# Layer 0's input transpose: from TensorE to a blocked load and a VectorE transpose

## The chip, the cores and the metric

The kernel runs on one core of one Trainium2 chip. The metric is device time in microseconds (us), and less is better. The core's engines are PE (TensorE, matrix multiplies and transposes), DVE (VectorE), ACT (ScalarE), POOL (GpSimd) and SP (SyncE, which here only issues DMAs). Each engine works through its own queue in order.

## The reference

64 graphs of 256 nodes with 256 features each pass through four graph layers; each layer's output is added to its input and normalised. In layer 0, which the change touches, x has the shape (64, 256, 256):

```python
q = proj(Wq, bq); k = proj(Wk, bk); v = proj(Wv, bv)     # x @ W.T + b, four heads of 64
attn = softmax(where(adj == 0, NEG, q @ k.T * 64 ** -0.5))
out = layer_norm((attn @ v) @ Wo.T + bo) * gamma + beta
x = layernorm(x + out)
```

Layer 1 is a second attention (eight heads of 32) with an MLP of width 1,024, layer 2 a graph attention with a rank-one score, and layer 3 a softmax over x * a0 @ x.T. All is computed in float32.

## The kernel before

The 64 graphs are worked on in 32 groups of two (G = 2, so T = 512 nodes, in TB = 4 blocks of 128 partitions). A group is a generator, `group(g)`, that issues some instructions and yields, about 45 times in all. A string, ORDER, says which group takes the next turn: in each of 32 periods the newest group takes its first turn, and older groups (up to five periods old) take theirs in between, so several groups at different layers are in work at once. FIRST and LAST are the same for the start and the end of the run. The program's order is made binding on PE alone (`in_order`); on the other engines a scheduler places instructions by when it expects their inputs, so an instruction there can move ahead of the turn that issued it.

The parts that matter here:

- `load_group(g)` issues two DMAs of 512 KB on SP, one for x (buffer `x0`, three buffers) and one for the integer adjacency `adj` (two buffers).
- `group(g)` casts `adj` to bf16 on ACT (L889), has four DMA transposes turn it (L897), and makes the mask on DVE (L900). `adjb`, the cast copy, has one buffer, so the next group's cast waits for this mask.
- `layer0` begins with `transposed(x)` (L577): for each of two halves of the features, four PE transposes of 128x128 (L531) go into one PSUM tile, and ACT copies it to `xT` (L584). Then PE computes q and k (`xT` as the moving operand) and v.
- `layer0` then has POOL add `beta0` to x in place (L717), because x is next needed in x + beta0. As it overwrites x, it waits for the PE transposes that read x. The sum is read at L744.
- `behind` in `layer0` normalises each graph twice. `stats` (L536) is a chain of DVE statistics (L544, L545), POOL additions (L547, L549) and a POOL power (L551). With `twice=True` two small DVE products follow (L553, L554). `scaled` (L557) then makes `z` on DVE (L559), once for each block of 128 nodes. In the instruction order they stand L553, L559 (first block of the graph), L554, L559 (second block), then L750, which makes `xb`.
- `layer1` starts with PE transposes of `z` (L758, again through L531), and multiplies exp(scores) by the mask on DVE, 32 instructions for each group (L613).

Tiles named `xT` share three buffers among five uses for each group. PSUM tiles named `pm` have four.

Of the kernel before, what the change touches and what calls it, by code (L numbers as in the profile page):

```python
# [8 lines left out]
F32 = mybir.dt.float32  # L9
BF16 = mybir.dt.bfloat16  # L10
I32 = mybir.dt.int32
# [5 lines left out]
P = 128  # L17
N = 256
D = 256
NC = D // P  # L20
G = 2
QB = N // P
TB = G * QB
T = G * N
# [376 lines left out]
def usual_input(ctx: ExitStack, tc: tile.TileContext, a: dict, out: bass.AP, flag: bass.AP):  # L401
# [7 lines left out]
    nc = tc.nc  # L409
# [3 lines left out]
    io = ctx.enter_context(tc.tile_pool(name="io", bufs=2))  # L413
    act = ctx.enter_context(tc.tile_pool(name="act", bufs=AT_ONCE))
# [24 lines left out]
    r_3 = const.tile([P, B // G, TB], F32, name="r_3")  # L439
    last = const.tile([P, B // G, TB], F32, name="last")  # L440

    def load_group(g):
        x0 = io.tile([P, TB, D], F32, name="x0", bufs=3)
        nc.sync.dma_start(x0, a["x"][g * G:(g + 1) * G].rearrange("b (q p) d -> p (b q) d", p=P))
        adj = io.tile([P, TB, N], I32, name="adj")
        nc.sync.dma_start(adj, a["adj"][g * G:(g + 1) * G].rearrange("b (q p) k -> p (b q) k", p=P))
        return x0, adj

    later = []

# [6 lines left out]
    def load_rows(name, cols, queue=None):  # L457

        src = a[name]
        t = const.tile([P, src.shape[0] // P, cols], F32, name=name)  # L460
        load(queue, t, src.rearrange("(c p) f -> p c f", p=P))
        return t
# [13 lines left out]
        return t  # L476


    first = load_group(0)
    wqT = load_rows("L0_gnn_WqT", D, nc.scalar)  # L480
    wkT = load_rows("L0_gnn_WkT", D, nc.scalar)
    bq = load_column(a["L0_gnn_bq"], D, "bq", nc.scalar)
# [44 lines left out]
    def matmul(*args, **kw):  # L527
        in_order(nc.tensor.matmul(*args, **kw))  # L528
# [38 lines left out]
    def tokens(gs):  # L567
        return slice(gs[0] * N, (gs[-1] + 1) * N)

    def to_psum(src, c, gs=ALL):  # L570

        pt = ps_m.tile([P, T], F32, name="pm")
        for t in blocks_of(gs):
            transpose(pt[:, t * P:(t + 1) * P], src[:, t, c * P:(c + 1) * P], ident)
        return pt

    def transposed(src, scale=None, bias=None, gs=ALL):  # L577

        on = tokens(gs)
        dst = act.tile([P, NC, T], F32, name="xT")  # L580
        for c in range(NC):
            pt = to_psum(src, c, gs)
            if scale is None:
                nc.scalar.copy(dst[:, c, on], pt[:, on])  # L584
            else:
                nc.scalar.activation(dst[:, c, on], pt[:, on], AF.Identity, bias=bias[:, c:c + 1], scale=scale[:, c:c + 1])  # L586
        return dst
# [92 lines left out]
    def project(dst, srcT, w, extra, row=None, gs=ALL):  # L680


        chunks = w.shape[1]
        for i in gs:
            pm = ps_m.tile([P, QB, D], F32, name="pm")
            if row is not None:
                matmul(pm, onesb, row.unsqueeze(1).to_broadcast([P, QB, D]), start=True, stop=False)
            for q in range(QB):
                t = i * QB + q
                for c in range(chunks):  # L690
                    matmul(pm[:, q, :], srcT[:, c, t * P:(t + 1) * P], w[:, c, :],
                           start=c == 0 and row is None, stop=c == chunks - 1 and (row is None or q == QB - 1))
                if chunks > NC:
                    yield
            o = dst[:, i * QB:(i + 1) * QB, :]
            if extra is None:
                nc.scalar.copy(o, pm)
            else:
                nc.vector.tensor_tensor(o, pm, extra[:, i * QB:(i + 1) * QB, 0:D], ALU.add)

    def layer0(g, x, mask):
        xT = transposed(x)
        yield
        qT = act.tile([P, NC, T], F32, name="qT")
        kT = act.tile([P, NC, T], F32, name="kT")
        for w, bcol, dst in ((wqT, bq, qT), (wkT, bk, kT)):
            for f in range(NC):
                pm = ps_m.tile([P, T], F32, name="pm")
                for c in range(NC):
                    matmul(pm, w[:, c, f * P:(f + 1) * P], xT[:, c, :], start=c == 0, stop=c == NC - 1)  # L710
                nc.scalar.activation(dst[:, f, :], pm, AF.Identity, bias=bcol[:, f:f + 1])
            yield
        v = act.tile([P, TB, D], F32, name="v")
        yield from project(v, xT, wvT, None)
        yield

        nc.gpsimd.tensor_tensor(x, x, over_blocks(beta0), ALU.add)  # L717
        y = act.tile([P, TB, D], F32, name="y")
        z = act.tile([P, TB, D], F32, name="z")
        xb = act.tile([P, TB, D], F32, name="xb", tag="v")  # L720

        def behind(i, oT, rz):

            rr = att.tile([P, NC, N], F32, name="rr")
            lines = dram.tile([NC, 2, N], F32, name="lines")

            queue = nc.sync if g else nc.gpsimd
            queue.dma_start(lines.rearrange("c h n -> (c h) n"), rz[0:P:32, :])
            for h in range(2):
                queue.dma_start(rr[h * 64:h * 64 + 64, :, :], lines[:, h, :].unsqueeze(0).to_broadcast([64, NC, N]))  # L730
            yield
            nc.vector.tensor_tensor(oT, oT, rr, ALU.mult)  # L732
            yield
            pm = ps_m.tile([P, QB, D], F32, name="pm")
            for q in range(QB):
                for c in range(NC):
                    matmul(pm[:, q, :], oT[:, c, q * P:(q + 1) * P], woT[:, c, :],
                           start=c == 0, stop=c == NC - 1)
            nc.vector.tensor_tensor(y[:, i * QB:(i + 1) * QB, :], pm, over_blocks(bop, QB), ALU.add)
            yield  # L740
            mv, rstd = stats(y, i)
            for q, t in enumerate(blocks(i)):
                nc.vector.scalar_tensor_tensor(y[:, t, :], y[:, t, :], mv[:, q, 0:1], gamma0, ALU.subtract, ALU.mult)  # L743
                nc.vector.scalar_tensor_tensor(y[:, t, :], y[:, t, :], rstd[:, 0, q:q + 1], x[:, t, :],  # L744
                                               ALU.mult, ALU.add)
            yield
            mv, rstd = stats(y, i, twice=True)
            scaled(z, y, i, mv, rstd[:, 1])
            for q, t in enumerate(blocks(i)):
                nc.vector.scalar_tensor_tensor(xb[:, t, :], z[:, t, :], rstd[:, 0, q:q + 1], beta1r, ALU.mult, ALU.add)  # L750
            yield

        yield from attention(qT, kT, v, mask, 64, None, behind, [r_0[:, g * G + i:g * G + i + 1] for i in range(G)])
        return xb, z
# [128 lines left out]
        return (yield from values_of(lambda i, kc, q: e[:, i, at[kc][q]:at[kc][q] + P], x, D, x, r_3[:, g], gs, last[:, g]))  # L883

    def group(g):
        x, adj = load_group(g) if g else first
        yield
        adjb = io.tile([P, TB, N], BF16, name="adjb", bufs=1)
        nc.scalar.activation(adjb, adj, AF.Copy, accum_out=there[:, g:g + 1])  # L889
        nc.scalar.activation(adj.bitcast(F32), adj, AF.Square, bias=minus_half, accum_out=edges[:, g:g + 1])  # L890
        yield


        pt = io.tile([P, G, QB, N], BF16, name="adjT", bufs=1)
        for t in range(TB):
            i, q = divmod(t, QB)
            nc.sync.dma_start_transpose(pt[:, i, :, q * P:(q + 1) * P], adjb[:, t, :])  # L897
        yield
        mask = act.tile([P, G, QB * N], BF16, name="mask")
        nc.vector.scalar_tensor_tensor(mask.rearrange("p g k -> p (g k)"), pt.rearrange("p g k q -> p (g k q)"), 1.0,  # L900
                                       adjb.rearrange("p t k -> p (t k)"), ALU.mult, ALU.min,
                                       accum_out=both_ways[:, g:g + 1])
        xb, z = yield from layer0(g, x, mask)
        y, hT, both = yield from layer1(xb, z, mask)

        def others(gs):

            yield from project(y, hT, w2, both, b2m, gs)
            x = yield from renormed(y, gs)
            x = yield from layer2(x, mask, gs)  # L910
            x = yield from layer3(g, x, mask, gs)
            i, j = g * G + gs[0], g * G + gs[-1] + 1
            nc.sync.dma_start(out[i:j].rearrange("b (q p) d -> p (b q) d", p=P), x[:, gs[0] * QB:(gs[-1] + 1) * QB, 0:D])

        if g < B // G - 1:
            yield from others(ALL)
            return

        parts = [others((i,)) for i in ALL]
        turn = 0  # L920
        while parts:
            for r in parts[:turn // QB + 1]:
                if next(r, END) == END:
                    parts.remove(r)
            turn += 1
            yield
# [77 lines left out]
    for period in range(len(groups)):  # L1004
        for age in ORDER:
            g = period - int(age)
# [61 lines left out]
```

## Time and profile before

| | |
|---|---|
| median of 3 runs | 2663.03 us (2661.43 to 2664.4) |
| profiled execution, first to last instruction (span) | 2658.2 us |
| PE busy | 2586.9 us, 97% of the span |
| DVE busy | 1965.7 us, 74% |
| ACT busy | 1293.9 us, 49% |
| POOL busy | 592.3 us, 22% |
| DMA queue of SP (q1) | 111,552 packets, 78.94 MB, 10.1% of 16 engines' span |

The profiled execution gives its span only, and no launch-to-end time of its own: the median of the runs lies 4.8 us above the span, and the profiled execution is read as a run of that length. Busy times of PE are modelled, and neighbouring matmuls overlap in them, so the time that a group of matmuls takes is read from start to start. In the lists of instructions below, columns are the start in us from the beginning of the span, the duration in us, engine, line, operation, output and inputs, shapes, and the count; a bracket gives the engine's idle time before it and what ended that.

### The profile page before, as it was taken

What the parts mean: (1) busy time and instruction counts of PE and PEld (TensorE: products, weight loads), DVE (VectorE), ACT (ScalarE), POOL (GpSimd) and SP (SyncE); (2) the same over time, 40 slices, a digit from 0 to 9 for tenths busy, and PEclk for the clock granted to TensorE, in tenths of its full rate; (3) what the DMA queues carried; (4) which work ended last, traced back from release to release, by engine and by line L of the source; (5) the groups of instructions that cost most, each with busy time, mean ns of one, the idle gap of its engine ahead of it and who ended that gap; (6) DMA issues with size and microseconds to landing.
All of it is one profiled execution on the core that took longest, in us unless ns stands there. A gap on an engine that the chain in (4) does not pass through costs nothing.

```text
span 2658.2 us, 44921 instructions
## 1 busy us (share of the span) xinstructions
PE 2586.9 (97%) x16648; PEld 1761.5 (66%) x16648; DVE 1965.7 (74%) x6189; ACT 1293.9 (49%) x1997; POOL 592.3 (22%) x1145
## 2 busy tenths in 40 slices
PE   6899999999999999999999999999999999999996
PEld 3567667666667666666676666676676676676665
DVE  4667777777777777777777777777777777777774
ACT  3445544545545545545455544555445455445442
POOL 2112222222222222222222222222222222222121
PEclk8999999999999999999999999999999999999998
DMA  6001011001010000010010110110110101000000
GB/s 163 25 9 32 26 37 37 25 29 29 29 37 29 33 29 28 29 37 27 28 36 25 33 37 25 29 37 21 36 37 25 29 29 29 29 21 17 17 1 25
DMA packets 113393, 83.20 MB, mean 31 GB/s; under 512 B 44304, under 2 KB 112656, under 8 KB 113168
## 3 DMA queue, kind: packets, MB, share of 16 engines
q1 hardware_dynamic: 111552, 78.94, 10.1%
q8 instruction: 134, 2.20, 0.4%
q10 hardware_dynamic: 1360, 0.79, 0.1%
q0 software_dynamic: 256, 0.53, 0.1%
q14 instruction: 91, 0.75, 0.1%
HBM read 54.80 MB, written 17.04 MB: 27 GB/s over the span
## 4 chain that ended last, share of the span: by engine, by line
PE 71%; DVE 17%; POOL 9%; issue 2%; DMA 1%; ACT 0%; SPq 0%; DVEq 0%; POOLq 0%; ACTq 0%
PE pm L528 55%; PE ps L528 10%; PE pm L531 7%; POOL rstd L551 6%; DVE st L544 3%; DVE y L816 2%; DVE y L744 2%; DVE xn L559 2%; POOL ve L547 2%; DVE z L559 2%; DVE mv L545 1%; DVE xb L750 1%; DVE y L743 1%; DVE r L815 1%; POOL ve L549 0%
## 5 line engine op out<-in xcount | busy, mean ns | idle before, releaser
L613 DVE SCALAR_TENSOR_TENSOR e<-e,mask 128x256 f32<-128x256 f32 x1024 | 428.2, 483 | 130.7 <-ACT e L605 130.7
L605 ACT ACTIVATE e<-ps 128x1024 f32<-128x1024 f32 x384 | 371.9, 1020 | 196.2 <-PE ps L528 176.3
L528 PE MATMUL pm<-L_gnn_W,hT 128*128 128x256 f32 x2048 | 463.0, 379 | 0.0
L528 PE MATMUL pm<-xT,L_gnn_W 128*128 128x512 f32 x1024 | 455.2, 592 | 0.0
L528 PEld LDWEIGHTS pm<-L_gnn_W,hT 128*128 128x128 f32 x2048 | 384.5, 190 | 49.2 <-issue 0.7
L788 ACT ACTIVATE hT<-pm,b 128x512 f32<-128x512 f32 x256 | 176.7, 691 | 408.1 <-PE pm L528 408.0
L528 PEld LDWEIGHTS pm<-xT,L_gnn_W 128*128 128x128 f32 x1024 | 191.7, 190 | 203.4 <-issue 198.5
L544 DVE BATCH_NORM_STATS2 st<-y 128x6 f32<-128x256 f32 x768 | 301.1, 408 | 6.7
L551 POOL TENSOR_TENSOR rstd<-ve,mhalf 128x2 f32<-128x2 f32 (+1 forms) x384 | 298.4, 777 | 26.7
L559 DVE TENSOR_SCALAR xn<-y,mv,rstd 128x256 f32<-128x256 f32 x384 | 141.9, 411 | 178.9 <-POOL rstd L551 178.8
L547 POOL TENSOR_SCALAR ve<-mv 128x2 f32<-128x2 f32 x384 | 98.9, 257 | 741.0 <-DVE mv L545 738.8
L774 POOL TENSOR_TENSOR both<-y,xb 128x512 f32<-128x512 f32 x64 | 81.4, 1272 | 764.2 <-DVE y L773 764.2
L607 DVE TENSOR_TENSOR e<-e,mask 128x1024 f32<-128x1024 f32 x128 | 150.8, 1221 | 15.3 <-ACT e L605 15.3
L528 PE MATMUL ps<-xT 32*128 32x256 f32 x2048 | 148.0, 402 | 2.2 <-ACT e L605 1.3
L586 ACT ACTIVATE xT<-pm,beta,gamma 128x512 f32<-128x512 f32 x128 | 92.3, 770 | 104.4 <-PE pm L531 104.3
L528 PE MATMUL pm<-e,z 128*32 128x256 f32 x2048 | 142.4, 387 | 0.3
L528 PEld LDWEIGHTS ps<-xT 32*128 32x128 f32 x2048 | 93.2, 185 | 74.0 <-issue 66.8
L528 PE MATMUL pm<-e,v 128*32 128x256 f32 x2048 | 125.4, 384 | 8.0 <-DVE e L607 8.0
L528 PE MATMUL pm<-L_gnn_WoT,oT 128*128 128x256 f32 x512 | 121.2, 391 | 8.3 <-DVE oT L732 6.0
L528 PE MATMUL ps<-qT,kT 64*128 64x256 f32 x1024 | 128.0, 389 | 0.5 <-ACT e L605 0.5
L528 PE MATMUL pm<-xT,L_gnn_WqT 128*128 128x512 f32 x256 | 120.9, 616 | 3.7 <-ACT xT L584 3.7
L816 DVE SCALAR_TENSOR_TENSOR y<-pm,r,xn 128x256 f32<-128x256 f32 x256 | 120.9, 473 | 2.5
(138 smaller groups left out, 4059.1 us busy)
## 6 DMA issues: line engine op xcount, KB each, us to landing
x<-in_x SPq DMA_DIRECT2D x32, 512.0 KB
adj<-in_adj SPq DMA_DIRECT2D x32, 512.0 KB
rr<-lines SPq DMA_DIRECT2D x124, 128.0 KB
out<-xn SPq DMA_DIRECT2D x31, 512.0 KB
adjT<-adjb SPq DMA_TRANSPOSE x128
L_gnn_W<-in_L_gnn_W SPq DMA_DIRECT2D x2, 1024.0 KB
lines<-zs SPq DMA_DIRECT2D x62, 4.0 KB
rr<-lines POOLq DMA_DIRECT2D x4, 128.0 KB, 3.3
```

Source lines behind the costliest of these rows:

```text
L528: in_order(nc.tensor.matmul(*args, **kw))
L531: in_order(nc.tensor.transpose(*args))
L544: nc.vector.bn_stats(st[:, q, :], src[:, t, 0:D])
L547: nc.gpsimd.tensor_scalar(ve[:, 0], mv[:, :, 1], EPS, None, ALU.add)
L551: nc.gpsimd.tensor_tensor(rstd, ve, mhalf[:, 0:k * QB].rearrange("p (k t) -> p k t", k=k), ALU.pow)
L559: nc.vector.tensor_scalar(dst[:, t, 0:D], src[:, t, 0:D], mv[:, q, 0:1], rstd[:, q:q + 1], ALU.subtract, ALU.mult)
L586: nc.scalar.activation(dst[:, c, on], pt[:, on], AF.Identity, bias=bias[:, c:c + 1], scale=scale[:, c:c + 1])
L605: nc.scalar.activation(e, ps, AF.Exp, scale=scale)
L607: nc.vector.tensor_tensor(e, e, mask.unsqueeze(1).to_broadcast([P, 2, QB * N]), ALU.mult)
L613: nc.vector.scalar_tensor_tensor(e[:, h, k], e[:, h, k], 1.0, mask[:, k], ALU.mult, ALU.mult, accum_out=sums[:, kc, c, j:j + 1])
L788: nc.scalar.activation(hT[:, f, :], pm, AF.Gelu, bias=b1[:, f:f + 1])
L816: nc.vector.scalar_tensor_tensor(y[:, t, :], po[:, 0:D], r, x[:, t, 0:D], ALU.mult, ALU.add)
```

## The change

`load_group` is split in two. `load_edges(g)` loads `adj`, now with one buffer, at the place where `load_group` stood. `load_x(g)` is called later, after the DMA transposes of `adj`. It loads x as before (now two buffers), and a second time in 32x32 blocks, by eight DMAs into `turned`, such that a transpose of each 32x32 block within its place gives `xT`. One DVE instruction does this for the whole group (128 partitions x 1,024 elements). The eight PE transposes and the two ACT copies of layer 0 are gone. Line numbers behind the edit move by 10 to 12: L528 becomes L538, L551 becomes L561, L553 L563, L559 L569, L613 L623, L717 L728.

```diff
-    def load_group(g):
-        x0 = io.tile([P, TB, D], F32, name="x0", bufs=3)
+    def load_edges(g):
+        adj = io.tile([P, TB, N], I32, name="adj", bufs=1)
+        nc.sync.dma_start(adj, a["adj"][g * G:(g + 1) * G].rearrange("b (q p) k -> p (b q) k", p=P))
+        return adj
+
+    def load_x(g):
+        turned = io.tile([P, NC, T // 32, 32], F32, name="turned", bufs=1)
+        rows = a["x"][g * G:(g + 1) * G].rearrange("b n d -> (b n) d")
+        parts = rows.rearrange("(t i) (c k j) -> k i c t j", i=32, c=NC, j=32)
+        for k in range(P // 32):
+            for c in range(NC):
+                nc.sync.dma_start(turned[32 * k:32 * k + 32, c], parts[k, :, c])
+        x0 = io.tile([P, TB, D], F32, name="x0")
         nc.sync.dma_start(x0, a["x"][g * G:(g + 1) * G].rearrange("b (q p) d -> p (b q) d", p=P))
-        adj = io.tile([P, TB, N], I32, name="adj")
-        nc.sync.dma_start(adj, a["adj"][g * G:(g + 1) * G].rearrange("b (q p) k -> p (b q) k", p=P))
-        return x0, adj
+        return x0, turned
...
-    first = load_group(0)
+    first = load_edges(0), load_x(0)
...
-    def layer0(g, x, mask):
-        xT = transposed(x)
+    def layer0(g, x, turned, mask):
+        xT = act.tile([P, NC, T], F32, name="xT")
+        nc.vector.transpose(xT.rearrange("p c t -> p (c t)"), turned.rearrange("p c t j -> p (c t j)"))
...
-        x, adj = load_group(g) if g else first
+        adj = load_edges(g) if g else first[0]
...
             nc.sync.dma_start_transpose(pt[:, i, :, q * P:(q + 1) * P], adjb[:, t, :])
+        x, turned = load_x(g) if g else first[1]
         yield
...
-        xb, z = yield from layer0(g, x, mask)
+        xb, z = yield from layer0(g, x, turned, mask)
```

## The prediction

> **What bounds the kernel now.** I read the page's busy shares first, then its chain of waits, then PE's list of waits, then one period as timelines.
>
> ```profile
> PE 2586.9 (97%) x16648; PEld 1761.5 (66%) x16648; DVE 1965.7 (74%) x6189; ACT 1293.9 (49%) x1997; POOL 592.3 (22%) x1145
> ...
> PE 71%; DVE 17%; POOL 9%; issue 2%; DMA 1%; ACT 0%; SPq 0%; DVEq 0%; POOLq 0%; ACTq 0%
> ```
>
> ```profile
> PE pm L531 <- DVE z L559: 9.2, 30, 0.7
> ```
>
> PE is full, yet a quarter of the chain lies on DVE and POOL. The second block (PE's waits: us in total, times, longest) tells why: 30 times, once a period, PE waits about 0.3 us for `z`. A period is 80.33 us from mask to mask (L900 at 775.14 and 855.5). In the chain, PE works without a gap from 772.4 to 831.8 us; from there to 772.4 us of the next period DVE and POOL run statistics, powers and scalings up to `z`, while PE has other work for all but 0.3 us of it. So two things lengthen a period one for one: PE's work between 772 and 832, and any delay of `z`. Here is that place, PE first, then DVE and POOL.
>
> ```profile
> 771.37 0.38 PE L531 MATMUL pm<-ident,z 128*128 128x128 f32 x2
> 772.05 1.16 PE L531 MATMUL pm<-ident,z 128*128 128x128 f32 x6 [0.29 <-DVE z L559]
> ...
> 781.35 1.04 PE L531 MATMUL pm<-ident,x 128*128 128x128 f32 x8
> 782.22 3.62 PE L528 MATMUL pm<-L_gnn_W,hT 128*128 128x256 f32 x16
> ```
>
> ```profile
> 771.51 0.16 DVE L553 TENSOR_TENSOR rstd<-rstd 128x2 f32<-128x2 f32 x1 [1.71 <-POOL rstd L551]
> 771.59 0.41 DVE L559 TENSOR_SCALAR z<-y,mv,rstd 128x256 f32<-128x256 f32 x1
> 771.91 0.15 DVE L554 TENSOR_TENSOR rstd<-rstd,ve 128x2 f32<-128x2 f32 x1
> 771.98 0.41 DVE L559 TENSOR_SCALAR z<-y,mv,rstd 128x256 f32<-128x256 f32 x1
> ...
> 775.14 1.23 DVE L900 SCALAR_TENSOR_TENSOR mask<-adjT,adjb 128x1024 bf16<-128x1024 bf16 x1
> ...
> 782.26 0.42 DVE L613 SCALAR_TENSOR_TENSOR e<-e,mask 128x256 f32<-128x256 f32 x1
> ...
> 782.61 2.56 DVE L613 SCALAR_TENSOR_TENSOR e<-e,mask 128x256 f32<-128x256 f32 x1
> ```
>
> ```profile
> 770.45 1.03 POOL L551 TENSOR_TENSOR rstd<-ve,mhalf 128x4 f32<-128x4 f32 x1
> ...
> 782.47 2.42 POOL L717 TENSOR_TENSOR x<-x,beta 128x1024 f32<-128x1024 f32 x1 [2.97 <-PE pm L531]
> ```
>
> The eight transposes of x begin at 781.35 and the next matmul at 782.22: they hold PE for 0.87 us, not the 1.04 of the record. They lie in the stretch that is PE alone. At 782.61 the eighth masking instruction takes 2.56 us where its neighbours take 0.42: it starts during POOL's addition of `beta0` and ends just after it (782.47 + 2.42 = 784.89; 785.17). This is no single case. L613's mean over 1,024 instructions is 483 ns on the page and its median 421: 62 ns x 1,024 = 63 us, as if some 30 of them lost 2.1 us each, once a group. Today the loss is harmless: DVE is done with this graph's masking at 785.18, and PE starts on the values at 786.85.
>
> [...]
>
> **The change, part by part.** It can be followed in the order in which each engine's queue stands once the changed program is built.
>
> 1. *PE loses eight transposes a group.* Nothing else moves in its queue. 0.87 us a period, on the path, in about 30 periods (the x transposes of the first two groups lie in the ramp): -26 us.
> 2. *ACT loses two copies a group* (592 ns each at the median). Nothing waited long for ACT here, and ACT is 49% busy: 0. If PE's work ahead of q did not cover them, this would be a gain.
> 3. *POOL's addition of `beta0` moves.* It waited for PE to have read x; now only for the load of x. In POOL's queue it now stands, for 30 of 32 groups, directly behind the power (L551, 770.45 to 771.48) that DVE's chain waits for. It is also another group's addition: that of the x which SP loads at 765.20, a period earlier than it is used. That x is there in time:
>
> ```profile
> 766.00:769.00 3.00, 3.00 (x19) 2.73 (x18) 1.61 (x8) 2.37 (x3) 1.44 (x3) 1.00 0.56 175
> 769.00:771.50 2.50, 2.50 (x14) 2.16 (x12) 0.81 (x4) 0.60 (x1) 1.44 (x3) 1.00 0.00 0
> ```
>
> (Windows of time: the last column is GB/s; 175 x 3 us = 525 KB, the whole 512 KB load, and nothing after 769.) With two buffers x still waits for the same read, L744 of two groups back, that it waits for today. So the addition starts as the power ends, at about 771.45, takes 2.34 to 2.42 us and ends near 773.8. DVE's L553 [...]comes at 771.51: it blocks, and both L559 and PE's transposes of `z` behind it. L553 then ends near 773.9 instead of 771.67: `z` is 2.25 us late. If L553 slips in first, L554[...] blocks instead, and the second half of `z` is as late. Bounds: 0[...] to 2.64, the longest L717 in the trace. I take 2.25. The first and the last periods have slack or no addition left: 28 x 2.25 = +63 us.
> 4. *The stall of L613 goes*: 2.15 us of DVE time a group, off the path. It pays for part 5.
> 5. *DVE gains one transpose of 128x1024 a group*, ahead of the mask. Nearest row: L607, 128x1024 in f32, 1.22 us. [...] I take 1.2. Behind it in DVE's queue wait the mask, then `y` (L699, 776.70), statistics, and the eight L613. With s its length, L613 ends 2.47 - s earlier after `z` than now; PE wants those 0.87 earlier after `z`, and has 1.67 to spare. The second L613 group has only 0.35, but starts from a PE result. Together they hide up to s = 2.65 us: 0 for 1.2[...]. Its `xT` buffer is free: PE's last read of the tile three allocations back comes before 766.
> 6. *SP issues eight more DMAs a group.* At 0.39 us (the x load of the same 512 pieces) that is 3 us, in a queue that idles from 784 to 813. Two of the eight stand ahead of the DMA transposes of `adj`, needed a period later. Data: 4,096 packets of 128 B; at the mean of 38.5 ns now (10.1% of 16 x 2658.2 us over 111,552 packets) 10 us on 16 engines[...]. They start near 780 and are wanted near 855: 0. `adj` in one buffer also has most of a period.
> 7. *Start.* The first group's blocks follow `adj` on SP (about 5 us of issue) and are turned on DVE; the second group's transpose stands behind a product that waits for a DMA until 52.2 us, while its q now starts at 44.9. Against that, `adj` comes first. I bound it by -4 and +8, and take +2.
>
> Sum: -26 + 63 + 2 = +39 us on the profiled execution's 2658.2 us, a period of 80.33 - 0.87 + 2.25 = 81.7. The same +39 on the median of 2663.0 gives 2702.
>
> **Rivals.** [...] If the addition starts late[...], `z` is on time and only parts 1 and 7 remain: 2663 - 26 + 2 = 2639. Against it: POOL, starting while one L613 ran, went ahead of the next one that already stood in the queue. It decides at a delay of 0.87 us (26 us / 30): below that the kernel gains. Chance 0.13. *The VectorE transpose is slow.* [...] deciding point s = 2.65 us. [...] Chance 0.06. *The blocks arrive late.* Their transpose would hold all of DVE's queue; it needs the eight DMAs to take over 70 us, seven times the estimate. Chance 0.02, 2720 and up. *A part of the delay only*, 0.8 to 0.95 us: no change, 2660 to 2668. Chance 0.02. That the PE transposes stay is excluded by its queue.
>
> **The numbers.** The case worked out has 0.77. Its own range: delay 2.0 to 2.6 us in 28 periods, 56 to 73, less 26, with the start from -4 to +8: 2689 to 2718. The range given, 2682 to 2730, adds a delay in a few periods more or fewer, and a transpose a little beyond its cover; it leaves out the fast rival and the slow transpose. A measurement of this kernel can tell about 0.2% (5 us) from no change. Faster 0.13, same 0.02, slower 0.85.
>
> **What would show it.** Right: PE's wait for `z` (now L569) at about 2.5 us, 28 times, some 70 us in all; L563 or L564 at 2.3 us instead of 0.15; POOL's addition (L728) directly behind the power; no long L623 any more; a DVE transpose of 1.2 us; 81.7 us from mask to mask. Wrong: L563 and L564 short and a period of 79.5 us (the first rival), or PE waiting for `e` (L623) behind a long transpose (the second).

## The result, and the profile after

| | before | after |
|---|---|---|
| median, 4 runs each on one chip | 2662.30 us (2661.43 to 2664.40) | 2709.14 us (2708.67 to 2710.23) |
| profiled execution, span | 2658.2 us | 2706.9 us |
| PE's mean granted clock | 0.992 | 0.987 |
| q1 (SP's DMAs) | 111,552 packets, 10.1% | 246,720 packets, 14.2% |

The changed kernel is slower: ratio 1.0177, 95% interval 1.0163 to 1.0191. Predicted were 2702 us and a range of 2682 to 2730. The medians differ by 46.8 us, the two spans by 48.7; the account below is made on the spans. The kernel before was profiled in a faster run than its median: where a run has both numbers, its time is about 2 us above its span (2708.67 and 2706.9 for the changed kernel), not 4.8 us, so the 2658.2 us stand for a run of some 2660 us, 2 below the median.

The page of the changed kernel, busy times and then the chain that ended last:

```profile
PE 2563.6 (95%) x16392; PEld 1741.2 (64%) x16392; DVE 1995.1 (74%) x6221; ACT 1260.0 (47%) x1933; POOL 588.1 (22%) x1145
...
PE 69%; DVE 19%; POOL 8%; issue 2%; DMA 1%; SPq 1%; ACT 0%; ACTq 0%; DVEq 0%; POOLq 0%
```

PE has 256 matmuls fewer and less busy time, and the span is longer: work was taken off the full engine, and PE is no longer full. DVE's part of the chain has grown from 17% to 19%. PE's waits in the changed kernel (us in total, times, longest) name the two places (L541 was L531, the transposes, and L538 was L528, the matrix multiplies):

```profile
PE pm L541 <- DVE z L569: 68.9, 30, 2.4
PE pm L538 <- DVE xT L713: 30.8, 2, 17.4
```

The wait for `z` stood at 9.2 us in 30 times before. It now takes 59.7 us more, and lasts up to 2.4 us once a period. Here is one such place in timelines of the changed kernel: PE, then DVE, then POOL.

```profile
376.95 0.38 PE L541 MATMUL pm<-ident,z 128*128 128x128 f32 x2
379.76 1.16 PE L541 MATMUL pm<-ident,z 128*128 128x128 f32 x6 [2.42 <-DVE z L569]
```

```profile
377.08 2.29 DVE L563 TENSOR_TENSOR rstd<-rstd 128x2 f32<-128x2 f32 x1 [1.71 <-POOL rstd L561]
379.30 0.40 DVE L569 TENSOR_SCALAR z<-y,mv,rstd 128x256 f32<-128x256 f32 x1
379.62 0.15 DVE L564 TENSOR_TENSOR rstd<-rstd,ve 128x2 f32<-128x2 f32 x1
```

```profile
376.02 1.03 POOL L561 TENSOR_TENSOR rstd<-ve,mhalf 128x4 f32<-128x4 f32 x1
377.02 2.34 POOL L728 TENSOR_TENSOR x<-x,beta 128x1024 f32<-128x1024 f32 x1
```

POOL's power ends at 377.05 and the addition of `beta0` follows at once. DVE's product of 128x2 starts 0.06 us after the addition, takes 2.29 us in place of 0.16, and ends at 379.37, just after the addition (379.36). PE's transposes stand still until then. The product is that of the second graph of the group; the first graph's, 3.5 us earlier, stays short. It happens in 30 of the 32 groups. In the first two PE does not wait for `z`; in the other 28 the wait lengthens the period.

Two more groups of the page: the masking, whose mean is now its median, so the stall has left it; and the new instruction.

```profile
L623 DVE SCALAR_TENSOR_TENSOR e<-e,mask 128x256 f32<-128x256 f32 x1024 | 363.9, 420 | 131.6 <-ACT e L615 131.6
L713 DVE STREAM_TRANSPOSE xT<-turned 128x1024 f32<-128x1024 f32 x32 | 39.6, 1237 | 12.1 <-DMA turned<-in_x 12.1
```

A period, taken from one group's first `z` to the next group's, is 81.58 us. Every fourth one is 82.9, which nothing in the prediction gives. Windows of time show where such a period differs (columns: window, its length, busy time and count of PE, weight load, DVE, ACT and POOL, PE's granted clock, DMA share, GB/s):

```profile
457.59:461.00 3.41, 1.32 (x8) 0.90 (x6) 2.34 (x2) 0.00 (x0) 3.34 (x2) 1.00 0.00 0
461.00:464.41 3.41, 3.07 (x10) 2.58 (x11) 3.38 (x9) 1.55 (x2) 0.00 (x0) 0.50 0.00 0
```

In the first window PE works for 1.32 of 3.41 us, as 2.1 us of the gap of 2.4 before `z` lie inside it. In the next one PE's granted clock is 0.50. That costs about 1.33 us (82.92 at the mean of the seven long periods, less 81.58), seven times. Before the change the clock did not fall at all between 112 and 2637 us.

The difference of 48.7 us, by the trace:

| | us |
|---|---|
| start: `z` of the second group at 127.6 in place of 122.0 | +5.6 |
| PE without the x transposes, 30 x (-0.9) | -27 |
| `z` 2.13 us late, 28 x 2.13 | +60 |
| 7 dips of the clock, 7 x 1.33 | +9 |
| end, and rest | +1 |

### The profile page after: what moved, and what is told of

It is laid out like the page before. It is cut to its first block, busy times and chain, and to the rows that moved or that the text cites. A ratio compares the mean times of both kernels' runs of the same rounds, so it can differ in the third digit from the quotient of the medians.

```text
span 2706.9 us, 44670 instructions
## 1 busy us (share of the span) xinstructions
PE 2563.6 (95%) x16392; PEld 1741.2 (64%) x16392; DVE 1995.1 (74%) x6221; ACT 1260.0 (47%) x1933; POOL 588.1 (22%) x1145
## 3 DMA queue, kind: packets, MB, share of 16 engines
q1 hardware_dynamic: 246720, 95.74, 14.2%
## 4 chain that ended last, share of the span: by engine, by line
PE 69%; DVE 19%; POOL 8%; issue 2%; DMA 1%; SPq 1%; ACT 0%; ACTq 0%; DVEq 0%; POOLq 0%
PE pm L538 54%; PE ps L538 9%; POOL rstd L561 6%; PE pm L541 6%; DVE st L554 3%; DVE rstd L563 3%; DVE y L827 2%; DVE y L755 2%; DVE xn L569 2%; POOL ve L557 2%; DVE z L569 1%; DVE mv L555 1%; DVE xb L761 1%; DVE y L754 1%; DVE r L826 1%
## 5 line engine op out<-in xcount | busy, mean ns | idle before, releaser
L615 ACT ACTIVATE e<-ps 128x1024 f32<-128x1024 f32 x384 | 371.9, 1020 | 224.6 <-PE ps L538 204.3
L538 PE MATMUL pm<-L_gnn_W,hT 128*128 128x256 f32 x2048 | 463.8, 382 | 0.0
L623 DVE SCALAR_TENSOR_TENSOR e<-e,mask 128x256 f32<-128x256 f32 x1024 | 363.9, 420 | 131.6 <-ACT e L615 131.6
L538 PE MATMUL pm<-xT,L_gnn_W 128*128 128x512 f32 x1024 | 455.1, 592 | 0.0
L538 PEld LDWEIGHTS pm<-L_gnn_W,hT 128*128 128x128 f32 x2048 | 391.7, 193 | 52.4 <-issue 0.7
L538 PEld LDWEIGHTS pm<-xT,L_gnn_W 128*128 128x128 f32 x1024 | 191.9, 190 | 203.2 <-issue 198.4
L561 POOL TENSOR_TENSOR rstd<-ve,mhalf 128x2 f32<-128x2 f32 (+1 forms) x384 | 298.3, 777 | 26.7
L569 DVE TENSOR_SCALAR xn<-y,mv,rstd 128x256 f32<-128x256 f32 x384 | 141.8, 411 | 178.4 <-POOL rstd L561 178.3
L538 PE MATMUL pm<-xT,L_gnn_WqT 128*128 128x512 f32 x256 | 121.8, 620 | 30.8 <-DVE xT L713 30.8
L538 PE MATMUL ps<-xT 32*128 32x256 f32 x2048 | 147.5, 400 | 2.2 <-ACT e L615 1.3
L563 DVE TENSOR_TENSOR rstd<-rstd 128x2 f32<-128x2 f32 x64 | 74.4, 1163 | 99.2 <-POOL rstd L561 99.2
L538 PE MATMUL pm<-e,z 128*32 128x256 f32 x2048 | 141.5, 385 | 0.4
L538 PEld LDWEIGHTS ps<-xT 32*128 32x128 f32 x2048 | 92.9, 184 | 73.5 <-issue 67.2
L538 PE MATMUL pm<-e,v 128*32 128x256 f32 x2048 | 126.0, 386 | 7.1 <-DVE e L617 7.1
L538 PE MATMUL ps<-qT,kT 64*128 64x256 f32 x1024 | 128.0, 389 | 0.5 <-ACT e L615 0.5
L538 PE MATMUL pm<-v,qT 128*128 128x260 f32 x512 | 119.6, 387 | 3.7 <-DVE qT L856 3.7
```

The lines of the kernel that those rows point to most:

```text
L561: nc.gpsimd.tensor_tensor(rstd, ve, mhalf[:, 0:k * QB].rearrange("p (k t) -> p k t", k=k), ALU.pow)
L563: nc.vector.tensor_tensor(rstd[:, 0], rstd[:, 0], rstd[:, 1], ALU.mult)
L569: nc.vector.tensor_scalar(dst[:, t, 0:D], src[:, t, 0:D], mv[:, q, 0:1], rstd[:, q:q + 1], ALU.subtract, ALU.mult)
L615: nc.scalar.activation(e, ps, AF.Exp, scale=scale)
L623: nc.vector.scalar_tensor_tensor(e[:, h, k], e[:, h, k], 1.0, mask[:, k], ALU.mult, ALU.mult, accum_out=sums[:, kc, c, j:j + 1])
```

## The experiments

I had one theory and several rivals. Theory: DVE's small product, right behind the power, is held up by POOL's addition (2.29 us in place of 0.16), and that is the loss; loads and VectorE transpose are hidden, and the dips follow from PE's gap. Rivals: the loads or the VectorE transpose cost the time; or DVE's chain is late for another reason. "Dips" are the stretches of half clock in the middle of the run, and a period runs from `z` to `z`. The ratios below are to runs of the kernel before on the same chip (medians of 2662.31 to 2663.21 us).

**The collision alone, without loads and VectorE transpose.** The kernel before, with the addition moved; so that it need not wait for PE it writes a buffer of its own, `xs`, which L744 then reads in place of x:

```diff
+            powers.append(power.ins.name)                    # of the group before
...
-        nc.gpsimd.tensor_tensor(x, x, over_blocks(beta0), ALU.add)
+        xs = io.tile([P, TB, D], F32, name="xs", bufs=1)
+        add = nc.gpsimd.tensor_tensor(xs, x, over_blocks(beta0), ALU.add)
+        if powers:
+            tc.add_manual_dep(add.ins, powers[-1], ...)      # order only
...
```

> The kernel before, with PE transposes and one load of x, and with one edit: the addition of beta0 writes a tile of its own, so that it need not wait for PE, and stands in POOL's queue directly behind the second power of the group before. If the place of the addition is the cause, the small product behind the power takes 2.3 us in some 30 groups, the period grows by 2.1 us to 82.5, and the run takes 2722 us, up to 2733 if PE's clock also dips. If the cause lies in the loads or the VectorE transpose, it stays at 2662 us.

Measured: 2738.18 us, ratio 1.0287 (1.0270 to 1.0305). PE's waits in this kernel:

```profile
PE pm L532 <- DVE z L562: 70.5, 30, 2.4
```

The period is 82.44 = 80.33 + 2.11, with 8 dips. So the addition's place alone gives the whole loss, dips included; 29 x 2.11 = 61, 8 x 1.7 = 13 for the dips and 2 at the start make up 76 of the 77 us by which the span grew. The total is 5 us above the most that was expected, 2733 with dips.

**The addition taken off POOL, all else as changed.**

```diff
-        nc.vector.transpose(xT..., turned...)
+        turn = nc.vector.transpose(xT..., turned...)
+        add = nc.vector.tensor_tensor(x, x, over_blocks(beta0), ALU.add)
+        tc.add_manual_dep(add.ins, turn.ins.name, ...)       # order only
...
-        nc.gpsimd.tensor_tensor(x, x, over_blocks(beta0), ALU.add)
```

> The changed kernel, with the addition of beta0 on VectorE, right behind the 32x32 transpose, in place of GpSimd. Nothing of GpSimd's then stands behind the power. [...] the product behind the power (L565 here) is short again, 0.16 us, PE's wait for z is back at about 9 us in all, no clock dips in the middle, a period of 80.33 - 0.87 = 79.46 us; VectorE's block of transpose and addition, 1.24 + about 1.2 us, stays within the cover of 2.65 us. The late start (5.6 us) stays: about 2663 + 5.6 - 26 = 2642, range 2636 to 2650. Rival (the place in time counts[...]: VectorE's chain is late whatever stands behind the power): a period near 81.6, 2700 or more. Second rival (the cover of 2.65 us is smaller than worked out): PE waits for e, up to 1.2 us a period, 2642 to 2680.

Measured: 2637.63 us, ratio 0.9905 (0.9890 to 0.9920), faster than both kernels. Its waits of PE, and a timeline of DVE:

```profile
PE pm L541 <- DVE z L569: 8.7, 30, 0.6
```

```profile
371.31 0.16 DVE L563 TENSOR_TENSOR rstd<-rstd 128x2 f32<-128x2 f32 x1 [1.70 <-POOL rstd L561]
...
374.83 1.24 DVE L713 STREAM_TRANSPOSE xT<-turned 128x1024 f32<-128x1024 f32 x1
375.99 1.18 DVE L913 SCALAR_TENSOR_TENSOR mask<-adjT,adjb 128x1024 bf16<-128x1024 bf16 x1
377.10 0.09 DVE L913 DVE_READ_ACCUMULATOR mask<-adjT,adjb 128x1 f32 x1
377.10 1.22 DVE L714 TENSOR_TENSOR x<-x,beta 128x1024 f32<-128x1024 f32 x1
```

The product is short again (163 ns at the longest of 64), no dip is left, and the period is 79.43, against 80.33 before. DVE does 32 additions of 1.22 us more and is busy for less (1966.5 us against 1995.1), as its 64 products take some 10 us together (0.161 at the median) in place of 74.4. The period's gain of 0.90 us is that of the x transposes, with loads, VectorE transpose and addition all on board: together these cost nothing in a period. The rivals "DVE's chain is late anyway" and "the loads or the VectorE transpose cost the time" are out. The addition stands behind the mask, so nothing of the mask waits for it.

**The addition on POOL, but later**, behind the group's k projection on PE:

```diff
+        k_done = on_pe[-1]
...
-        nc.gpsimd.tensor_tensor(x, x, over_blocks(beta0), ALU.add)
+        add = nc.gpsimd.tensor_tensor(x, x, over_blocks(beta0), ALU.add)
+        tc.add_manual_dep(add.ins, k_done, ...)              # waits for it
```

> The changed kernel, with one edit: POOL's addition of beta0 waits for the last matmul of the group's own k projection, where DVE has a gap; nothing else moves. [...] L563 is back at 0.16 us, PE's wait for z at about 0.3 us a period, the period at 80.33 - 0.87 = 79.5 us, and the run at 2662 - 26 + 6 (start) = about 2641 us, faster than before the change. If the eight DMAs, the VectorE transpose or the queue of SP cost the time instead, it stays near 2709 us.

Measured: 2675.26 us, ratio 1.0048 (1.0031 to 1.0064). That is 34 us more than was expected. The wait for `z` is 9.1 us again, without dips, but the period is 80.64, not 79.46. The addition met another of DVE's instructions (POOL's line first, then DVE's), and PE now waits for `e`:

```profile
485.40 2.46 POOL L729 TENSOR_TENSOR x<-x,beta 128x1024 f32<-128x1024 f32 x1 [11.32 <-PE pm L541]
```

```profile
485.56 2.57 DVE L623 SCALAR_TENSOR_TENSOR e<-e,mask 128x256 f32<-128x256 f32 x1
```

```profile
PE pm L538 <- DVE e L617: 32.2, 32, 6.2
```

The same block of DVE costs 2.13 us a period in front of `z`, about 1.2 here, and nothing in the kernel before. I had taken this place for free, and it isn't. Of the 1.2 us, about 0.8 show as PE's longer wait for `e` (32.2 us against 7.1 in the changed kernel, over 30 periods). ACT's exponentials (L615) wait 16.1 us for L623, in 30 times, where in the changed kernel they never do; how the rest of the 1.2 us comes about is open.

**The addition cut in four, and in two**, at its place on POOL (the diff is for four; in two, each instruction takes two blocks):

```diff
-        nc.gpsimd.tensor_tensor(x, x, over_blocks(beta0), ALU.add)
+        for t in range(TB):
+            nc.gpsimd.tensor_tensor(x[:, t, :], x[:, t, :], beta0, ALU.add)
```

> The changed kernel with GpSimd's addition of beta0 in four instructions of 128x256 (about 0.6 us each) in place of one of 128x1024, at the same place behind the power. If a VectorE instruction waits for the one GpSimd instruction [...] and then goes ahead, L563 waits for the first piece (ends 0.6 us after the power) and L564, which comes 0.57 us later, for the second (1.2 us): L563 about 0.6 us, the second half of z about 1.0 us late in place of 2.13. Period 79.46 + 0.45 to 1.0 = 79.9 to 80.5, no clock dips, 2642 + 28 x 0.45 to 1.0 = 2655 to 2670. Rival [...]: L563 at 2.3 us, period 81.6 with dips, 2709.

> The same addition in two instructions of 128x512 (about 1.2 us each). L563 waits for the first, L564 for the second, so the second half of z is as late as in the changed kernel (about 2.1 us), but PE's gap is in two parts of about 1.1 us with two transposes between. Period 81.5. If a dip of the granted clock needs one gap of over 2 us, there are none: 2709 - 9 = 2700, range 2695 to 2705. If it needs only the sum of idle time, 7 dips stay: 2709. If L564 isn't blocked (the second piece too late), period 80.5 and 2671.

Measured: 2707.76 us in four (ratio 1.0177, 1.0163 to 1.0191) and 2709.58 us in two (1.0178, 1.0164 to 1.0192): no gain that the intervals would show, although DVE's instructions come in between POOL's pieces. With four pieces, POOL's line and then DVE's:

```profile
377.48 2.81 POOL L729 TENSOR_TENSOR x<-x,beta 128x256 f32<-128x256 f32 x4
```

```profile
377.54 0.68 DVE L563 TENSOR_TENSOR rstd<-rstd 128x2 f32<-128x2 f32 x1 [1.70 <-POOL rstd L561]
378.14 0.89 DVE L569 TENSOR_SCALAR z<-y,mv,rstd 128x256 f32<-128x256 f32 x1
378.96 0.68 DVE L564 TENSOR_TENSOR rstd<-rstd,ve 128x2 f32<-128x2 f32 x1
379.56 0.89 DVE L569 TENSOR_SCALAR z<-y,mv,rstd 128x256 f32<-128x256 f32 x1
```

By these times the two engines take turns: with 2.81 / 4 = 0.70 us for a piece, an estimate, the pieces end at 378.18, 378.89, 379.59 and 380.29, and DVE's four instructions end 0.04 to 0.16 us after one each, at 378.22, 379.03, 379.64 and 380.45. So L569 waits too (0.89 us in place of 0.41, in 60 of its 128 executions for `z`), which the expectation had left out. The four waits add up to 2.0 us, nearly the old stall of 2.13, and the period is 81.46. In two pieces L563 takes 1.22 us and the first L569 takes 1.43, and PE's gap stays in one piece of 2.4 us, so this run (8 dips) tells nothing of divided gaps; the one in four pieces does, with 9 dips and no gap over 1.3 us.

**More VectorE transposes**, the same one done twice and four times:

```diff
+        for _ in range(2):                                # or 4
             nc.vector.transpose(xT..., turned...)
```

> The changed kernel with the VectorE transpose done twice, so 2.47 us a group in place of 1.24. By the cover of 2.65 us worked out for the prediction, nothing is added: 2709, range 2705 to 2716. If VectorE has no cover left, 1.24 us x 30 = +37: 2746, which is what four times measured.

> The changed kernel, with the VectorE transpose made four times in a row (4.7 us instead of 1.24 us for each group). By the prediction's count DVE's slack behind z hides 2.65 us; the rest, 2.0 us a period, is lost: PE waits for e (L623), and the run takes about 2709 + 59 = 2768 us. If DVE's queue is not near the path there, it stays at 2709; if each transpose is on the path in full, it is 3.5 us a group, 2820 us.

Measured: twice 2711.77 us (ratio 1.0184, 1.0170 to 1.0198, within the interval of the changed kernel), with a period of 81.59 and 7 dips as there. Four times 2746.41 us (1.0314, 1.0297 to 1.0332): +37, not +59, with a period of 82.64 outside the dips, so 1.06 us more, and 16 dips. DVE's cover holds to at least 2.47 us, as worked out; beyond it, three more transposes of 1.23 us cost less than expected, with DVE's instructions partly in another order. PE's weight loads then wait 25.8 us for `e` (L623), against 6.0 in the changed kernel, so it is the place that was expected. The VectorE transpose is not what the change loses by.

**The gap filled with PE work**, identity transposes into the tile that the transposes of `z` overwrite, just ahead of these:

```diff
     def to_psum(src, c, gs=ALL, fill=0):
...
+        for _ in range(fill):
+            transpose(pt[:, 0:P], ident, ident)
...
-        zT = transposed(z, gamma1, beta1)
+        zT = transposed(z, gamma1, beta1, fill=20)       # or 16
```

> The changed kernel, with 20 transposes of the identity on PE ahead of each group's transposes of z: 2.2 us of useless work in the gap in which PE waits for z. If the lower clock seen in every fourth period (3.4 us at half speed, 1.33 us lost) comes from PE standing idle there, it is gone, all periods take 81.6 us, and the run takes 9 us less, about 2700 us. If it has another cause[...], the dips stay, and the run is at 2709 us or more, up to 2775 if the added work cannot hide.

> The changed kernel with 16 transposes of the identity on PE, into the PSUM tile that the transposes of z then overwrite, just ahead of these: they fill most of PE's gap of 2.3 us before z. ACT's order is that of the changed kernel; on VectorE only the 32x32 transpose moves behind the mask. If the dips of the granted clock (every fourth period, 1.33 us each) come from that gap, they are gone and all else stays: a period of 81.6 without exception, 2709 - 9 = 2700, range 2696 to 2706. If they come from something else, they stay: 2709 or more, as the fill costs what the gap doesn't cover.

Measured: with 20, 2757.85 us (1.0357, 1.0340 to 1.0374), a miss: the dips are gone, but the scheduler put ACT's `xT` copies behind another group's cast, PE waited for them (46.0 us in 30 times) and the period is 83.28. Its time says nothing of the gap. With 16, where ACT's order stays, 2706.36 us (1.0163, 1.0150 to 1.0177). PE's waits with 16:

```profile
PE pm L541 <- DVE z L569: 19.7, 28, 0.7
```

The period is 81.60 from the third group to the last but one, and no dip is left. From the third group's `z` to the last one's it takes 2365.3 us against 2373.1 in the changed kernel, 7.8 less; 5.1 of these go again at the start and 1.1 at the end, and the total is 0.4 above the expected range. So the gap makes the dips; the two medians alone, with intervals that overlap, would not have shown it.

**The first two groups as before**, on top of the addition on DVE: x loaded plainly and first, PE transposes, POOL's addition.

```diff
-    first = load_edges(0), load_x(0)
+    first = load_plain(0), load_edges(0)
...
+        if turned is None:
+            xT = transposed(x)
+            nc.gpsimd.tensor_tensor(x, x, over_blocks(beta0), ALU.add)
```

> As the kernel with the addition on VectorE, but the first two groups load x plainly, first of all, and are transposed on PE with GpSimd's addition, as before the change. If the late start of the changed kernel comes from the blocks of the first two groups, PE's two waits for xT of 13 and 17 us are gone and z of the second group comes near 131 us instead of 136: 2663 - 26 = 2637, range 2631 to 2644, about 5 below the kernel with the addition on VectorE alone. If the start is late for another reason (the order of adj and x on SP), no difference from that kernel: 2642.

Measured: 2637.23 us, ratio 0.9904 (0.9889 to 0.9919): the same as without it. The two waits for `xT` are gone and the second group's `z` comes at 123.4 us, against 126.1 (and 122.0 before). PE's transposes of it, which the expectation counted, begin at 132.4 in place of 134.9. So the late start comes from the way in which the first two groups get x. As this run also puts x ahead of `adj` again, it doesn't tell the blocks from the order of the loads. Of the 2.7 us gained there, 1.3 are lost in the periods and 1.0 at the end; why was not settled.

**The loads alone**, in the kernel before, into a buffer that nothing reads (and `adj` in one buffer):

```diff
+        load_turned(g)          # the eight DMAs, behind the DMA transposes of adj
```

> The kernel before, with the eight blocked DMAs for each group added behind the DMA transposes of adj, into a buffer that nothing reads, and adj in one buffer; PE transposes, ACT copies and GpSimd's addition as before. Nothing waits for the eight: a period of 80.33 and 2663, range 2659 to 2668, if they are hidden, as the prediction has it. If SP's queue is too full or the DMA engines contend (weights, rr and lines late): over 80.5 a period, 2668 or more.

Measured: 2673.70 us, ratio 1.0047 (1.0034 to 1.0061), as high as the second case of the expectation had it (2668 or more), but not by a longer period, and not the test it was meant to be. As nothing reads the buffer, nothing holds the loads back: SP had issued those of all 32 groups by 486 us, for instance

```profile
305.77 23.00 SPq L455 DMA_DIRECT2D turned<-in_x  x28
```

(SP's queue; start and time taken.) PE waited for `oT`, which needs `rr` from the same queue, up to 4.7 us at a time, and the sixth group's `z` was 13.7 us late. After that the period is 80.32, but no such loads are left in it. That loads spread over the periods cost nothing is shown by the kernel with the addition on DVE, not by this one.

## Why the prediction was right

1. *PE loses eight transposes: -26.* Right: 80.33 to 79.43 us a period with the addition on DVE, -0.90 for the 0.87 read from start to start. From the second group's `z` to the third's, and from the last but one to the last, PE has no longer wait for `z` in the changed kernel, and these two periods show the same: 82.88 against 83.77, and 79.44 against 80.33.
2. *ACT's copies: 0.* No other term is left in a period of 79.43.
3. *POOL's addition blocks DVE behind the power: +63.* Right in place, line and count. Read from L563 (2.29 less 0.16) and from PE's waits (59.7 / 28), `z` is 2.13 us late, where I took 2.25: 28 x 2.13 = 60. It was L563 all 30 times, never L564, and its 2.29 to 2.31 us are nearly the whole of the addition (2.34 to 2.36). That it would be held up as L613 was (2.56 us) was an estimate before the run.
4. *The stall of L613 goes.* Right: 420 ns at the mean, 483 before.
5. *The VectorE transpose: 0.* Right. 1,237 ns, as the nearest row had it (1.22 us). The cover of 2.65 us held at 1.24 and at 2.47 us; that it ends there was not shown. Its working does not come out of the numbers that it gives: for the first masking group they leave 2.47 + 1.67 - 0.87 = 3.27, and how the second group's 0.35 makes this 2.65 isn't said. Four transposes, 4.7 us, cost 1.06 us a period; one for one that would be a cover of about 3.6, an estimate, as DVE's order differs there.
6. *SP and the blocks: 0.* Right in the periods. The added 135,168 packets took about 1,850 us on 16 engines together (14.2% of 16 x 2706.9 us less 10.1% of 16 x 2658.2), about 14 ns for each, where the mean before was 38.5, with which the prediction counted.
7. *Start: +2.* This term was mis-sized: +5.6, inside its bounds of -4 and +8. PE waits 30.8 us for the first two `xT`, where before it waited 5.7 us for x and 3.7 for ACT's copies. With the addition on DVE, so without the first group's collision (at 76 us), the start is 4.1 late.

The term that the sum lacked is the clock: part 3 priced PE's gap at its length only, and behind seven of the gaps of 2.4 us the clock was at 0.50 for 3.41 us, +9. Too little for the clock and the start (+13) and 3 too much for the delay make most of the difference between +39 and +48.7. Of the rivals, the first, with `z` on time, is excluded by L563 (2.29 us); the slow transpose and late blocks by the kernel with the addition on DVE. What the first rival priced, 2639, is what that kernel reaches (2637.6).

## What to carry to other kernels

An operation's wait also holds its place: when a change takes away the input that an off-path instruction waited for, see where it goes in its queue, and beside which instruction of another engine it then runs: here L563 took 2.29 us beside it in place of 0.16. The same 2.3 us of blocking cost nothing, 1.2 or 2.1 us a period by its place alone, and cutting the operation in pieces did not help; giving it to the engine that it was blocking did (2709 to 2638 us). PE's gap cost its length and what the clock did behind it: the gap grew by 2.1 us, and the clock took 1.33 more in every fourth period.

## What the hardware showed that was not expected

**Half clock behind short gaps.** In the trace of the changed kernel each of the seven dips has a granted clock of 0.50 for 3.41 us, and they start 327.68 us apart (461.03, 788.71, 1116.39 us and on), which is four periods and the loss of one dip (4 x 81.58 + 1.33 = 327.65) and 96 times the length of a dip. With the middle of the run laid out in stretches of that length, on which the dips fall, and PE's gaps added up in each, the stretches ahead of the seven dips have 2.12 to 2.22 us idle, and all others in the middle at most 1.88; in the run with four pieces, where no gap is longer than 1.3 us but two follow each other, 1.84 to 1.93 against at most 1.47. In the run with the collision alone they overlap (1.77 to 2.27 against at most 1.90), and some matmul records may be missing, so no limit that holds for all three runs can be read from these sums.

They do show why it is every fourth period. The gap is as long each time (2.42 to 2.44 us), but the part of it in the stretch in which it begins grows: for the four gaps from 541.8 us on it is 1.16, 1.50, 1.83 and 2.18 us, and behind the fourth comes a dip. A period is 24 stretches less 0.34 us (81.92 - 81.58), so the gap begins 0.34 us earlier in its stretch each time; the 1.33 us of the dip then move it 0.99 later again. With four pieces the dip comes in every third period.

**DVE and POOL take turns.** In the run in four pieces DVE's L563, L569, L564 and L569 took 0.68, 0.89, 0.68 and 0.89 us beside POOL's four pieces, where for the group's first graph they take 0.16, 0.41, 0.15 and 0.40. Together they wait 2.0 us, nearly the 2.13 that L563 waits beside the addition in one piece, and that is why cutting it up gained nothing.
